# Two graph layers in one kernel: order of layer-norm biases, opening sums, the closing of the last score chain, one load of the diagonal, and where the W1 evacuations stand

## The chip, the cores and the metric

The kernel runs on one core of one Trainium2 chip, in fp32. The metric is device time in microseconds (us), the median of three runs. The profile is of one further execution.

## The reference

Two layers over a graph of 3327 nodes (padded to 26 tiles of 128 rows, 3328) with 512 features and a dense 3327 x 3327 adjacency `adj`:

```
h = relu(layernorm(x));  q = h Wq' + bq;  k = h Wk' + bk;  v = h Wv' + bv
x = x + softmax(q k' / sqrt(512) + adj + adj) v            # layer 0
h = relu(layernorm(x));  A2 = adj + I;  d = diag(A2) ** -0.5
x = x + relu((d A2 d) (A2 h W1'))                           # layer 1
```

## The kernel before, in words

All large matrix products are done in the form of Strassen and Winograd: seven products of half size in place of eight, with sums and differences of blocks made on VectorE. Nodes are split in two halves of 13 tiles (`HALF`), columns in two strips `s` of 14 and 12 tiles (widths `Q` of 448 and 384 in one product). The name of a product (`p1` to `p7`, `m1`) says which blocks it multiplies.

Stage 1, row tiles (to about 110 us). For each tile of x, `norm` (L186) makes statistics on VectorE (`bn_stats` L191, `bn_aggr` L195, `ve` L197), the power -0.5 on GpSimd (L199) and the bias on VectorE (`nb`, L203). ScalarE makes relu(scale x + bias) (`ht`, L321), TensorE transposes it (`tp`, L330) into one of two PSUM banks, ScalarE copies the transposed blocks out (L339 for a tile of the first half, L341 for one of the second), and for the second half VectorE adds blocks (L346, L347). A bank is free again when its copy and its additions are done. `after(ins, other)` gives the builder's scheduler an order on one engine without a semaphore. `adds_of(n)` names the additions of the tile at least three places back in the row order, and `norm` puts the statistics behind them. Between the transposes TensorE makes the projections of q (`project_q`, L451, the merged weight `M`).

Stage 2, scores (about 110 to 622 us). 52 pairs of row tiles: 4 groups (strip and half of the queries) of 13. A pair is a `Chain` of seven products into PSUM rings X, Y and Z (L653); VectorE adds each product into the adjacency tiles g0, g1 (`first` L657, `more` L665), ScalarE takes the exponential (L660, L667), SyncE writes the parts to DRAM (`pd`). A chain's last product, p4, is run in the middle of the next chain (`Chain.finish`), so that it has its bank. Beside each product a fixed list `beside_of(k)` of further work for VectorE is run: the sums s1 to s4 (L675 to L688), `gather` (L699), and the adjacency sums of the next pair (L639, diagonal L643). The block is under `in_order`, which keeps the written order on VectorE, TensorE, GpSimd and SyncE. `at_score[k]` holds loads that are put ahead of pair k.

Stage 3, three large products, `steps`: for g = 0 (softmax times h), 1 and 2 (A2 times something), for each of seven products r, each strip s, seven `t` (six pairs of tiles and one single tile). One step has seven matmuls (L1052) or four (L1043), and needs `a` (loaded by `Step.load`, L1008 and others, three steps ahead), its block sums `o` (`four_sums`, L164 to L166, two steps ahead) and the right side `b` (`Right`, L731, L756, L171 to L174). The views `part` take the memory of `hp`, which the scores read. The loads of steps 0 to 2 and the sums of steps 0 and 1 are written after the scores' block, outside any `in_order`, so the scheduler places them. Between steps further tasks run, put at a step's number by `at(k, what)`; their parts wait in a list `waiting`, of which `run` (L1421 on) lets two go after each matmul while W1 products are inserted. Among these tasks: `totals` and `place_totals` (the softmax sums), `prepare` (Wv, bv and the diagonal `dg`), `prepared` (d from `dg`), `load_diagonal` and `scales` (d again, in blocks of 32 rows, `by_32`, wanted in the last product by `Columns.scale`), `judge` and `judged` (a flag for whether the softmax sums are in range). While step (1, 5, 1, 2) and on run, `Temp.product` (L1220) multiplies by W1: seven small products into two halves of one bank, emptied by ScalarE (L1224) or VectorE (L1226).

The lines above are those of the kernel before. In the kernel after, lines shift by a few (`norm` by 1, the scores by 6), and `left` and `Step` stand ahead of the scores' block.

Of the kernel before, what the change touches and what calls it, by code (L numbers as in the profile page):

```python
# [47 lines left out]
def graph_layers_kernel(  # L48
# [98 lines left out]
    by_32 = const.tile([P, NP // 32], F32, name="by_32")  # L147

# [39 lines left out]
    def norm(src, kept=None, behind=None):  # L188

        st = small.tile([P, 6], F32, name="st")  # L190
        ins = nc.vector.bn_stats(st, src)  # L191
        if behind:
            after(ins, behind)
        mv = small.tile([P, 2], F32, name="mv") if kept is None else kept
        nc.vector.bn_aggr(mv, st)  # L195
        ve = small.tile([P, 1], F32, name="ve")
        nc.vector.tensor_scalar(ve, mv[:, 1:2], EPS, None, op0=ALU.add)  # L197
        rstd = small.tile([P, 1], F32, name="rstd") if kept is None else kept[:, 1:2]
        nc.gpsimd.tensor_tensor(rstd, ve, mhalf, op=ALU.pow)  # L199

        def bias():
            nb = small.tile([P, 1], F32, name="nb")
            nc.vector.scalar_tensor_tensor(nb, mv[:, 0:1], -1.0, rstd, op0=ALU.mult, op1=ALU.mult)  # L203
            return nb

        return rstd, bias
# [107 lines left out]
    def opened(i, behind=None):  # L314
        fetch_x([j for _, j in order].index(i) + 9)
        xt = first.pop(i)
        return xt, *norm(xt, behind=behind)
# [34 lines left out]
    def adds_of(n):  # L352

        return next((summed_up[i] for _, i in reversed(order[: n - 3]) if i in summed_up), None)

    def h_transposed(k, done={}):

        for n, (kk, i) in enumerate(order):
# [4 lines left out]
            else:  # L363
                ht = normal(i, *opened(i, adds_of(n)), behind=taken[order[n - 3][1]])
# [6 lines left out]
    class Turned:  # L371


        def __init__(self, k):
# [3 lines left out]
            for m, (kk, i) in enumerate(order):  # L378
# [4 lines left out]
                rstd, bias = norm(xt, stats[:, :, i // HALF * n + i % HALF - a], adds_of(m))  # L383
# [236 lines left out]
    class Pair:  # L620
# [26 lines left out]
        def multiply(self, qt):  # L647
# [16 lines left out]
            def more(n, ps):  # L664
                nc.vector.tensor_add(a[n], a[n], ps[:, :wd])  # L665
                if n == 1:
                    nc.scalar.activation(g[0], g[0], AF.Exp)  # L667
# [109 lines left out]
    pairs = {}  # L777
    fours = mid(12, [P, 2, Q[0]], "s4")
    steps = [(n, t) for n in range(len(groups)) for t in range(HALF)]

    def fetch(k):
        if k < len(steps):
            pairs[k] = Pair(*steps[k])

    def beside_of(k):
        def on(j, what, *args):
            if 0 <= j < len(steps):
                getattr(pairs[j], what)(*args)

        def difference():  # L790
            if k < len(steps) and steps[k][1] >= 6:
                next(more_of, None)

        return (
            lambda: (on(k - 2, "s4"), on(k - 2, "gather", 0)),
            lambda: (on(k - 1, "s3"), on(k - 2, "gather", 1)),
            lambda: on(k + 1, "sum_of_adjacency", 0),
            lambda: on(k + 1, "sum_of_adjacency", 1),
            lambda: (on(k - 2, "total", 0), difference()),
            lambda: (on(k - 2, "total", 1), on(k - 1, "s1"), next(ahead, None) if k in making else None),  # L800
            lambda: (on(k - 1, "s2"), next(ahead, None) if k in making else None),
        )

    coming = queries(0)
    for ins in more_queries(0, coming):
        if ins:
            after(ins, parts_made[-1])
    for k in range(2):
        fetch(k)
    for m in range(2):  # L810
        pairs[0].sum_of_adjacency(m)
    more_of = iter(())
    with in_order(*(e.engine for e in (nc.vector, nc.tensor, nc.gpsimd, nc.sync))):
        for k, (n, t) in enumerate(steps):
            for what in at_score.get(k, ()):
                what()
            if t == 0:
                qt = coming
            fetch(k + 2)
            if t == 2 and n + 1 < len(groups):  # L820
                coming = queries(n + 1)
                more_of = more_queries(n + 1, coming)
            beside = beside_of(k)
            pairs[k].multiply(qt)
        k = len(steps)
        beside = beside_of(k)
        for what in beside[:2]:
            what()
        Chain.finish()
        for what in (*beside[5:], *beside_of(k + 1)[:2]):  # L830
            what()
        for _ in ahead:
            pass

    def totals():
        for m in range(2):
            pairs[len(steps_of_scores) - 1].total(m)
        for s in range(2):
            y0, y1 = (by_32[:, 4 * (STRIPS[s] + y * HT[s]) : 4 * (STRIPS[s] + (y + 1) * HT[s])] for y in range(2))
            nc.vector.tensor_sub(y0, y0, y1)  # L840

    def place_totals():
        tiled = job_ring([P, P], "tiled")
        for k in range(P // 32):
            nc.vector.tensor_reduce(tiled[:, 32 * k : 32 * k + 32], ident.rearrange("p (a e) -> p e a", e=32), axis=AX.X, op=ALU.add)
        ps = bank(ROLE["p8"], "tot")[:, : 4 * NT]
        nc.tensor.matmul(ps, tiled, by_32, start=True, stop=True)
        ps = ps.rearrange("p (i a) -> p i a", a=4)
        for a in range(4):
            nc.scalar.copy(tot[32 * a : 32 * a + 32, :], ps[32 * a : 32 * a + 32, :, a])  # L850

    steps_of_scores = steps

    ROLE = {"p1": 0, "p6": 2, "p7": 4, "p5": 6, "p2": 7, "p3": 1, "p4": 5, "p8": 3}

    def banks_for(*names):
        return {r: bank(ROLE[r], r) for r in names}

    verdict = []

    def judge():

        if N < NP:
            other = small.tile([P, 1], F32, name="other")
            nc.vector.tensor_sub(other, tot[:, NT - 2 : NT - 1], tot[:, NT - 1 :])
            nc.vector.scalar_tensor_tensor(tot[:, NT - 1 :], other, padding, tot[:, NT - 1 :], op0=ALU.mult, op1=ALU.add)
        within = small.tile([P, NT], F32, name="within")
        nc.vector.tensor_scalar(within, tot, SMALL, None, op0=ALU.is_ge)  # L870
        good = small.tile([P, NT], F32, name="good")
        nc.vector.scalar_tensor_tensor(good, tot, LARGE, within, op0=ALU.is_le, op1=ALU.mult)
        most = small.tile([P, 2], F32, name="most")
        nc.vector.tensor_reduce(most[:, 0:1], tot, axis=AX.X, op=ALU.max)
        nc.vector.tensor_reduce(most[:, 1:2], tot, axis=AX.X, op=ALU.min)
        ps = bank(ROLE["p8"], "p8")
        nc.tensor.matmul(ps[:1, :NT], ones, good, start=True, stop=True)
        for k in range(2):
            nc.tensor.transpose(ps[:1, (k + 1) * P : (k + 2) * P], most[:, k : k + 1], ident)
        verdict.append(ps)  # L880

    def judged():
        ps, one = verdict[0], small.tile([1, 4], F32, name="one")
        nc.vector.reduce_sum(one[:, 0:1], ps[:1, :NT], axis=AX.X)
        nc.vector.tensor_reduce(one[:, 1:2], ps[:1, P : 2 * P], axis=AX.X, op=ALU.max)
        nc.vector.tensor_reduce(one[:, 2:3], ps[:1, 2 * P : 3 * P], axis=AX.X, op=ALU.min)

        nc.vector.scalar_tensor_tensor(one[:, 3:4], one[:, 2:3], RATIO, one[:, 1:2], op0=ALU.mult, op1=ALU.is_ge)
        nc.vector.scalar_tensor_tensor(one[:, 3:4], one[:, 0:1], NT * P - 0.5, one[:, 3:4], op0=ALU.is_ge, op1=ALU.mult)
        nc.vector.tensor_scalar(bad, one[:, 3:4], 0.5, None, op0=ALU.is_lt)  # L890

    sd = const.tile([P, NT], F32, name="sd")
    rs = const.tile([P, NT], F32, name="rs")

    def weights(src):

        w = [half(k, [P, 2, D], "w") for k in (12, 13)]
        for c in range(DC):
            nc.sync.dma_start(w[c // 2][:, c % 2], src[c * P : (c + 1) * P])
        return [w[c // 2][:, c % 2] for c in range(DC)]  # L900

    LD = adjT.shape[1]
    mh = const.tile([P, NT], F32, name="mh")
    nc.vector.memset(mh, -0.5)
    dg = const.tile([P, NT], F32, name="dg")
    bvs = []

    def prepare():
        wv_w1.append(weights(wvT))
        bvs.append(half(11, [P, D], "bv_sb"))  # L910
        nc.sync.dma_start(bvs[0], bass.AP(tensor=bv.tensor, offset=bv.offset, ap=[[0, P], [1, D]]))
        with nc.allow_non_contiguous_dma(reason="the diagonal, once"):
            nc.sync.dma_start(dg, bass.AP(tensor=adjT.tensor, offset=adjT.offset, ap=[[LD + 1, P], [P * (LD + 1), NT]]))

    def load_diagonal():
        with nc.allow_non_contiguous_dma(reason="the diagonal, once"):
            for a in range(4):
# [957 lines left out]
```

## Time and profile before

| | us |
|---|---|
| runs | 2147.93, 2149.40, 2150.25 (median 2149.4) |
| profiled execution | 2149.21 |
| its span, first to last instruction | 2147.4 |
| TensorE granted clock, mean | 0.999 |
| DMA moved | 592 MB, mean 276 GB/s |
| VectorE waiting for DMA of `part` from `p` (13 times) | 26.1 |

The page gives for each engine its busy time, share of the span and number of instructions. Views of the trace are: waits (who waited for whom, in total, times, longest), the timeline (start, length, engine, line, operation, output <- inputs, count of merged instructions; in brackets the idle time before and what ended it), and windows (busy time of each engine in a stretch, then clock, DMA share and GB/s). PE is TensorE's matmul, PEld its weight load, DVE VectorE, ACT ScalarE, POOL GpSimd, SP SyncE. Line numbers are those of the kernel.

### The profile page before, as it was taken

What the parts mean: (1) busy time and instruction counts of PE and PEld (TensorE: products, weight loads), DVE (VectorE), ACT (ScalarE), POOL (GpSimd) and SP (SyncE); (2) the same over time, 40 slices, a digit from 0 to 9 for tenths busy, and PEclk for the clock granted to TensorE, in tenths of its full rate; (3) what the DMA queues carried; (4) which work ended last, traced back from release to release, by engine and by line L of the source; (5) the groups of instructions that cost most, each with busy time, mean ns of one, the idle gap of its engine ahead of it and who ended that gap; (6) DMA issues with size and microseconds to landing.
All of it is one profiled execution on the core that took longest, in us unless ns stands there. A gap on an engine that the chain in (4) does not pass through costs nothing.

```text
span 2147.4 us, 20866 instructions
## 1 busy us (share of the span) xinstructions
PE 2136.9 (100%) x6272; PEld 1180.7 (55%) x6272; DVE 1642.7 (76%) x3214; ACT 273.9 (13%) x441; POOL 68.7 (3%) x63
## 2 busy tenths in 40 slices
PE   9999999999999999999999999999999999999998
PEld 6555555555555555555454555555666665555554
DVE  7579888888887678776777777887466666688888
ACT  6312211112110000001111000000111100000000
POOL 2000000000003000000111000000000000000000
PEclk9999999999999999999999999999999999999999
DMA  8678888888999899888788889886646677978897
GB/s 299 218 258 303 298 312 284 303 291 295 326 339 310 286 350 328 282 303 302 262 310 295 302 284 340 309 314 225 198 157 215 180 212 238 289 225 248 268 280 194
DMA packets 402929, 592.09 MB, mean 276 GB/s; under 512 B 140012, under 2 KB 274296, under 8 KB 402808
## 3 DMA queue, kind: packets, MB, share of 16 engines
q1 hardware_dynamic: 371464, 527.61, 74.6%
q10 hardware_dynamic: 31344, 63.06, 8.0%
q8 instruction: 52, 0.85, 0.2%
q14 instruction: 69, 0.57, 0.1%
HBM read 417.60 MB, written 178.98 MB: 278 GB/s over the span
## 4 chain that ended last, share of the span: by engine, by line
PE 95%; DVE 2%; DMA 2%; issue 0%; ACT 0%; ACTq 0%; SPq 0%; POOL 0%; DVEq 0%
PE p L1052 56%; PE Y L653 13%; PE Z L653 6%; PE p L1043 5%; PE p L1159 4%; PE pw L1220 4%; PE X L653 3%; PE Y L451 2%; PE Z L451 1%; PE X L451 1%; DMA p<-g 0%; DMA bq_sb<-in_bq_dram 0%; DMA part<-p 0%; DMA rows<-row 0%; PE tp L330 0%
## 5 line engine op out<-in xcount | busy, mean ns | idle before, releaser
L1052 PE MATMUL p<-part,b 128*128 128x448 f32 (+1 forms) x3528 | 1257.6, 513 | 0.1
L1052 PEld LDWEIGHTS p<-part,b 128*128 128x128 f32 x3528 | 669.9, 190 | 541.2 <-issue 292.9
L164 DVE TENSOR_TENSOR part<-part 128x896 f32<-128x896 f32 (+1 forms) x252 | 256.5, 1018 | 71.1 <-DMA part<-p 26.1
L653 PE MATMUL Y<-qt,hp 128*128 128x448 f32 (+1 forms) x832 | 308.7, 513 | 0.7 <-DVE g L657 0.6
L653 PEld LDWEIGHTS Y<-qt,hp 128*128 128x128 f32 x832 | 157.7, 190 | 135.0 <-issue 72.8
L653 PE MATMUL Z<-qt,hp 128*128 128x384 f32 (+1 forms) x416 | 162.2, 512 | 0.0
L166 DVE TENSOR_TENSOR part<-part,part 128x448 f32<-128x448 f32 (+1 forms) x219 | 129.4, 591 | 15.0
L165 DVE TENSOR_TENSOR part<-part,part 128x448 f32<-128x448 f32 (+1 forms) x219 | 129.4, 591 | 7.3
L1043 PE MATMUL p<-part,b 128*128 128x448 f32 (+1 forms) x336 | 124.2, 512 | 0.0
L653 PEld LDWEIGHTS Z<-qt,hp 128*128 128x128 f32 x416 | 79.0, 190 | 66.2 <-issue 37.9
L657 DVE SCALAR_TENSOR_TENSOR g<-g,Y 128x384 f32<-128x384 f32 (+1 forms) x156 | 91.4, 586 | 30.5 <-PE Y L653 29.1
L1095 ACT COPY part<-p 128x384 f32<-128x384 f32 (+1 forms) x33 | 16.6, 502 | 658.4 <-PE p L1052 554.9
L1043 PEld LDWEIGHTS p<-part,b 128*128 128x128 f32 x336 | 63.8, 190 | 54.1 <-issue 31.4
L660 ACT ACTIVATE g<-g 128x768 f32<-128x768 f32 (+1 forms) x48 | 43.0, 896 | 346.5 <-DVE g L657 273.5
L653 PE MATMUL X<-qt,hp 128*128 128x384 f32 (+1 forms) x208 | 81.1, 512 | 0.0
L1096 DVE TENSOR_TENSOR part<-p,part 128x384 f32<-128x384 f32 (+1 forms) x33 | 19.3, 586 | 69.5 <-PE p L1052 65.5
L1159 PE MATMUL p<-w,ct 128*128 128x512 f32 x136 | 61.6, 592 | 0.0
L1115 DVE TENSOR_TENSOR ct<-p,part 128x448 f32<-128x448 f32 (+1 forms) x72 | 43.1, 610 | 21.5 <-PE p L1043 16.3
L653 PEld LDWEIGHTS X<-qt,hp 128*128 128x128 f32 x208 | 39.5, 190 | 33.1 <-issue 19.3
L199 POOL TENSOR_TENSOR rstd<-ve,mhalf 128x1 f32<-128x1 f32 x46 | 39.6, 862 | 535.6 <-DVE ve L197 527.0
L1220 PE MATMUL pw<-w,rows 128*128 128x256 f32 x208 | 53.4, 379 | 0.0
L1150 DVE TENSOR_TENSOR job<-job 128x896 f32<-128x896 f32 (+1 forms) x52 | 52.9, 1017 | 0.1
(192 smaller groups left out, 1664.6 us busy)
## 6 DMA issues: line engine op xcount, KB each, us to landing
part<-sum SPq DMA_DIRECT2D x104, 448.0 KB, 4.9
part<-p SPq DMA_DIRECT2D x91, 448.0 KB, 6.1
part<-sum SPq DMA_DIRECT2D x104, 384.0 KB, 3.8
part<-p SPq DMA_DIRECT2D x91, 384.0 KB, 4.3
part<-in_adjT_dram SPq DMA_DIRECT2D x78, 448.0 KB, 4.9
b<-row SPq DMA_DIRECT2D x234, 128.0 KB, 4.8
part<-in_adjT_dram SPq DMA_DIRECT2D x78, 384.0 KB, 3.9
g<-in_adjT_dram SPq DMA_DIRECT2D x52, 448.0 KB, 4.3
```

Source lines behind the costliest of these rows:

```text
L164: yield nc.vector.tensor_add(o[:, 0:2], g[:, 0:4:3], g[:, 1:2].to_broadcast([P, 2, g.shape[-1]]))
L165: yield nc.vector.tensor_add(o[:, 2], o[:, 1], g[:, 0])
L166: yield nc.vector.tensor_add(o[:, 3], o[:, 2], g[:, 2])
L451: nc.tensor.matmul(ps[:, :w], M[B[name]][:, c, o * P : (o + 1) * P], hp[k][:, A[name], c], start=start and c == 0, stop=c == 1, skip_group ...
L653: nc.tensor.matmul(ps[:, :wd], h_of(self.t, name, k), qt[B[name]][:, k], start=start and k == 0, stop=k == 1, skip_group_check=True)
L657: nc.vector.scalar_tensor_tensor(a[n], a[n], 2.0, ps[:, :wd], op0=ALU.mult, op1=ALU.add if sign > 0 else ALU.subtract)
L1043: yield nc.tensor.matmul(ps[("p2", "p3", "p4", "p8")[k]][:, :w], b[:, z], a[:, 0, y], start=k == 3 and not self.seeded, stop=True, skip_gr ...
L1052: yield nc.tensor.matmul(ps[r][:, :w], b[:, i], m, start=self.t == 0 and not adds, stop=self.t == PAIRS - 1 and r in ("p1", "p5", "p6", "p ...
L1115: nc.vector.tensor_tensor(o, p[k], c, op=ALU.subtract if k == "p3" else ALU.add)
L1150: nc.vector.tensor_add(self.a, self.a, self.b)
L1159: nc.tensor.matmul(ps, cts[s][y][d][:, k * P : (k + 1) * P], w[d], start=d == 0, stop=d == DC - 1)
L1220: nc.tensor.matmul(ps, a, W[B[name]][:, c], start=new and c == 0, stop=c == 1, skip_group_check=True)
```

## The change

- `norm` takes two instructions to stand behind: one for the statistics, one for the bias. For tiles from place 13 in the order, the statistics stand behind the additions of the tile five back, the bias behind those three back.
- `left`, `Step`, `view` and the rings move ahead of the scores. The loads of steps 0, 1 and 2 are put at pairs 44, 45 and 46. The six sums of steps 0 and 1 are put at named places of pairs 47 to 51 (`opens`).
- After the scores, `Chain.finish()` comes first, then VectorE's rest.
- `dg` is loaded once, by ScalarE's queue behind an exponential at pair 20. `load_diagonal` of `by_32` (four DMAs), and `scales`, are gone; `place_scales` copies `sd` into `by_32` by 16 ScalarE copies at step 12.
- `prepare` (Wv, bv) moves from step 2 to step (0, 4, 1, 1), number 64. The reductions for `place_totals` move one step up, the verdict's matmuls and the reading of them one step down.
- In `run`, one waiting part instead of two is let go after the second matmul, where a W1 product follows at place 3.

```diff
-    def norm(src, kept=None, behind=None):
+    def norm(src, kept=None, behind=(None, None)):
...
-        if behind:
-            after(ins, behind)
+        if behind[0]:
+            after(ins, behind[0])
...
-            nc.vector.scalar_tensor_tensor(nb, mv[:, 0:1], -1.0, rstd, op0=ALU.mult, op1=ALU.mult)
+            ins = nc.vector.scalar_tensor_tensor(nb, mv[:, 0:1], -1.0, rstd, op0=ALU.mult, op1=ALU.mult)
+            if behind[1]:
+                after(ins, behind[1])
...
-    def adds_of(n):
+    def adds_of(n, back=3):
-        return next((summed_up[i] for _, i in reversed(order[: n - 3]) if i in summed_up), None)
+        return next((summed_up[i] for _, i in reversed(order[: n - back]) if i in summed_up), None)
+    def behind_of(n):
+        return (adds_of(n, 5), adds_of(n)) if n >= HALF else (adds_of(n), None)
...
+    openers = [Step(0, ORDER[0], 0, t, right) for t, right in enumerate(ahead_of)]
+    for n, step in enumerate(openers):
+        at_score.setdefault(44 + n, []).append(step.load)
+    def sums_of_openers():
+        for step in openers[:2]:
+            yield from step.sums()
+    opens, opening = ((47, 4), (48, 4), (49, 4), (50, 4), (51, 2), (51, 3)), sums_of_openers()
...
+    def load_diagonal():
+        step = adjT.shape[1] + 1
+        with nc.allow_non_contiguous_dma(reason="the diagonal, once"):
+            after(nc.scalar.dma_start(dg, bass.AP(tensor=adjT.tensor, offset=adjT.offset, ap=[[step, P], [P * step, NT]])), Pair.exp)
+    at_score.setdefault(20, []).append(load_diagonal)
...
-            lambda: on(k + 1, "sum_of_adjacency", 0),
-            lambda: on(k + 1, "sum_of_adjacency", 1),
-            lambda: (on(k - 2, "total", 0), difference()),
+            lambda: (on(k + 1, "sum_of_adjacency", 0), open_up(2)),
+            lambda: (on(k + 1, "sum_of_adjacency", 1), open_up(3)),
+            lambda: (on(k - 2, "total", 0), difference(), open_up(4)),
...
-        beside = beside_of(k)
-        for what in beside[:2]:
+        Chain.finish()
+        for what in (*beside_of(k)[:2], *beside_of(k)[5:], *beside_of(k + 1)[:2]):
             what()
-        Chain.finish()
-        for what in (*beside[5:], *beside_of(k + 1)[:2]):
-            what()
...
-    def scales():
-        nc.vector.tensor_scalar(by_32, by_32, 1.0, None, op0=ALU.add)
-        nc.gpsimd.tensor_tensor(by_32, by_32, mhalf.to_broadcast(by_32.shape), op=ALU.pow)
+    def place_scales():
+        for a in range(4):
+            to = by_32[32 * a : 32 * a + 32].rearrange("p (i b) -> p b i", b=4)
+            for b in range(4):
+                nc.scalar.copy(to[:, b], sd[32 * b : 32 * b + 32])
...
-    for k, what in ((1, totals), (3, place_totals), (2, prepare), (6, prepared), (5, load_diagonal), (11, scales), (8, judge), (9, judged)):
+    for k, what in ((1, totals), (2, tile_identity), (3, place_totals), (6, prepared), (8, judge), (9, judge_sums), (10, judged),
+                    (12, place_scales), (number_of(0, 4, 1, 1), prepare)):
...
-                do(first_of(waiting), 2)
+                do(first_of(waiting), 1 if j == 2 and (k, 3) in inserted else 2)
```

## The prediction

> **What bounds the kernel now.** I read the page's busy row first, then the waits of TensorE, then the timelines at those waits.
>
> ```profile
> PE 2136.9 (100%) x6272; PEld 1180.7 (55%) x6272; DVE 1642.7 (76%) x3214; ACT 273.9 (13%) x441; POOL 68.7 (3%) x63
> ```
>
> TensorE is never free for long, and the clock row is 9 in all 40 slices. The edits add and remove no matmul, so nothing is to be had but the moments in which TensorE waits. The view of its waits lists few, since it counts idle time after modelled ends:
>
> ```profile
> PE tp L330 <- ACT hp L339: 1.0, 1, 1.0
> PE Y L653 <- DVE g L657: 0.6, 2, 0.3
> PE p L877 <- DVE most L874: 0.5, 1, 0.5
> ```
>
> So I took starts from the timeline instead. Undisturbed passes start every 0.322 us (384 columns), 0.376 (448), 0.216 (256) and 0.109 (transposes); an fp32 matmul is two passes. What a start lies beyond that is lost, and a disturbed pass is mostly followed by 0.10 more. Over the span this gives about 8 us in intervals of more than 0.06. Of it 1.8 is the warm-up on zeros, 0.4 the first projections, 0.4 one wait at 1127.8; none of these is touched. The rest, 5.53 us, is in four places, and each edit aims at one.
>
> Place A, row tiles (26 to 62 us): 0.25 at 34.66, 1.21 at 48.20, 0.09 at 51.78, sum 1.55. TensorE first, then ScalarE:
>
> ```profile
> 46.35 0.81 PE L451 MATMUL Z<-hp,M 128*128 128x384 f32 x2
> 48.20 0.63 PE L330 MATMUL tp<-ident,ht 128*128 128x128 f32 x4 [1.05 <-ACT hp L339]
> ```
>
> ```profile
> 46.92 0.81 ACT L321 ACTIVATE ht<-xt,nb,rstd 128x512 f32<-128x512 f32 x1 [0.56 <-DVE nb L203]
> 47.64 0.56 ACT L339 COPY hp<-tp 128x512 f32<-128x512 f32 x1
> ```
>
> Two passes from 46.35 end their turn at 46.99; the transpose started 1.21 later, when its bank had been copied. The copy stood behind an activation that waited for a bias, whose statistics had been held behind the additions of the tile three back.
>
> Place B, the last five pairs of scores (583 to 623): 0.34, 0.61, 0.38, 0.49, then 0.21 at the first products, sum 2.02. VectorE, then TensorE:
>
> ```profile
> 577.85 0.62 DVE L165 TENSOR_TENSOR part<-part,part 128x448 f32<-128x448 f32 x1
> 579.98 1.09 DVE L164 TENSOR_TENSOR part<-part 128x896 f32<-128x896 f32 x1 [1.52 <-DMA part<-p]
> ```
>
> ```profile
> 588.34 3.23 PE L653 MATMUL Y<-qt,hp 128*128 128x384 f32 x8 [0.34 <-DVE g L657]
> 599.52 1.56 PE L653 MATMUL Y<-qt,hp 128*128 128x384 f32 x4 [0.22 <-DVE g L657]
> ```
>
> An addition of the opening product was put on VectorE before its load (issued at 574.0) had landed. VectorE stood 1.52, then worked without a gap from 580.99 to past 600, and TensorE waited for banks that VectorE reads.
>
> Place C, the verdict, 0.75: two passes of L877 and the transposes started when VectorE's L874/L875 were done.
>
> ```profile
> 663.86 0.21 PE L877 MATMUL p<-good,ones 128*1 128x26 f32 x2 [0.50 <-DVE most L874]
> ```
>
> Place D, times W1 (1572 to 1690): 0.08, 0.08, 0.10, 0.24, 0.36, 0.35, sum 1.21. VectorE, then TensorE:
>
> ```profile
> 1671.38 0.62 DVE L166 TENSOR_TENSOR part<-part,part 128x448 f32<-128x448 f32 x1
> 1671.92 0.68 DVE L756 TENSOR_TENSOR b<-rows 128x512 f32<-128x512 f32 x1
> 1672.52 0.48 DVE L1226 SCALAR_TENSOR_TENSOR ts<-pw,sd,ts 128x256 f32<-128x256 f32 x1
> ```
>
> ```profile
> 1671.30 1.67 PE L1052 MATMUL p<-part,b 128*128 128x448 f32 x4
> 1673.06 1.13 PE L1220 MATMUL pw<-w,ct 128*128 128x256 f32 x4
> ```
>
> The last W1 product was due at 1671.30 + 4 x 0.376 = 1672.81; it needs the half bank that L1226 empties, and L1226 stood behind L756.
>
> **The change, part by part.** Beside the trace I use the order of instructions per engine, as both kernels build.
>
> *D.* In each such step L1226 moves ahead of one addition (L756 or L166: 0.60 to 0.68 from start to start). At 1672 it then starts at 1671.92 and ends at 1672.40, before 1672.81; the largest lateness was 0.25. All go: **1.21** (lower bound 0.9 if a bank release trails). The addition is later by 0.40 and feeds a step two further on, some 10 us.
>
> *C.* The verdict's matmuls go one step later, behind seven products (4.5 us), VectorE's part stays. **0.75**. Its reading by VectorE moves a step too; nobody waits for the flag before the end.
>
> *A.* For the later tiles the statistics are tied behind additions five back, the bias behind three back. I walked the new order with the trace's steps: statistics 0.60, aggregate 0.11, small ones 0.08, additions 0.33 each, activation 0.72, big copy 0.48, half copy 0.28. At 32.71 VectorE now takes two statistics (1.20) ahead of the additions that free a transpose bank; these end at 35.3 instead of 34.51, the transpose comes at 35.46 where it was due at 35.05 (the second Z matmul now precedes it): 0.41 lost instead of 0.25. The 1.21 goes: the activation is ready at 45.75 instead of 46.92, the copy at 46.0, just when TensorE wants the bank. What is late next is the last transpose: its bank's additions wait for a ScalarE copy that stands behind an activation and a projection's copy, and end at 50.3, where TensorE was there at 50.0; with the latency some 0.45. Left 0.9, so gain **0.65**; bounds -0.2 (both lates grow by 0.5) and 1.4.
>
> *B.* Opening sums of steps 0 and 1 stand now at named places of pairs 47 to 51, their loads at pairs 44 to 46, 27 us ahead. The DMA wait of 1.52 is gone. VectorE's step is 0.465 for the 384-wide operations, 0.54 and 1.00 for the sums, 0.21 for a diagonal: pairs 47 and 48 end without lag in their 9.03 us. But the sums of step 2, which the change doesn't name, still float into pairs 49 and 50 in the new order. There VectorE has 9.9 us of work in 9.03. Walking it, the release of the bank for the seventh product of pair 50 ends 0.2 before TensorE wants it; pair 51 has no adjacency sums and catches up. So four waits (1.81) go. The last chain is closed sooner, with two products (1.5 us) ahead of its last matmul, which takes 0.1 away. Then product p3 needs that chain's bank, and its release now stands behind two sums of step 3 (1.5 us, the first waiting for product p5): it would end at about 0.25 after p3 is due, with the restart 0.35 to 0.45. I take 0.45 left in B in all: gain **1.57**, bounds 0.7 (two more waits) and 1.9.
>
> *The diagonal.* Four transfers into `by` (L918), the addition L922 and GpSimd's 17 us are removed, 16 ScalarE copies added, `dg` moves from SP to ScalarE's queue in pair 20, Wv and bv (five loads) to a step near 930 us. Copies: L850 has 0.17 to 0.19 for the same shape, 2.9 us together; ScalarE is 13% busy and nothing behind them there is wanted for tens of us: 0 (2.9 if something were). The `dg` issue took 0.43 on SP, one of L918 took 5.64; it sits between ScalarE's exponentials at 299.0 and 306.75, a gap of 7.7: 0. The transfers themselves:
>
> ```profile
> 557.00:566.00 9.00, 9.00 (x30) 5.29 (x29) 7.87 (x19) 1.69 (x2) 0.00 (x0) 1.00 0.99 338
> 566.00:575.00 9.00, 9.00 (x30) 5.29 (x29) 8.68 (x19) 1.69 (x2) 0.00 (x0) 1.00 0.91 316
> 646.00:654.00 8.00, 8.00 (x23) 4.08 (x22) 5.09 (x9) 0.53 (x1) 0.00 (x0) 1.00 0.98 34
> ```
>
> (Last two columns: DMA share and GB/s.) While L918's 13,312 single elements ran, 34 GB/s moved in 8 us. TensorE lost nothing there, so their removal gives 0. `dg` is a quarter, some 2.3 us of engine time. Read by the row alone, a queue was blocked, and ScalarE's own queue would spare the g loads. The Trainium skill ("DMA: Bandwidth & Descriptors", section "Issuing engines are not separate DMA queues") speaks against that: whichever engine issues, the transfers interleave on the same 16 engines, and only issue time is saved. By the row the g loads lose 0, by the rule up to 2.3; a g tile issued at 568.88 lands 4.3 later (the page's median) and is first read at 575.76, so 2.6 is spare. Either way 0, upper bound 0.5. Wv and bv, 1.3 MB at a share of 0.75 to 1.0, go against loads three steps ahead (15 us): 0.
>
> **Sum.** 1.21 + 0.75 + 0.65 + 1.57 = 4.18. The profiled execution took 2149.21 (span 2147.4 and 1.8 around it): 2145.03. The median, 2149.4, is 0.2 from it, inside its runs' spread, so I keep **2145.0**.
>
> **Rivals.**
> *Everything named is recovered* (A and B without remainder): 5.5 us, 2143.7. For it: pair 50 has the 0.75 of an inserted product as extra room. Against: VectorE's order in A. Chance 0.22.
> *A new wait takes the old one's place*: A gains nothing, p3 and pairs 49 and 50 wait for VectorE: 1.21 + 0.75 + 0.7, 2146.5; the overload of 0.9 in two pairs speaks for it. Chance 0.13.
> *Slower, by DMA in pairs 44 to 46*: two loads of 448 KB instead of one stand ahead of the g loads in SP's queue, at shares of 0.85 to 1.0. Each pair adds 1.3 us of transfer at 350 GB/s; the spare shares are 1.35, 0.1 and 0.8 us, so 1.7 piles up, below the 2.6 of g and 1.8 of VectorE's lead. It decides once g lands 4.4 later than now. Then each of three pairs waits for what is beyond; at a pile of 7, about 2.6 each, 7.8 against 4.2 gained: 2152.8. Chance 0.07.
> *It doesn't do what it says* (the builder's order floats on): 0 to 1, 2149. Chance 0.03.
>
> **How the numbers follow.** A measurement of this kernel tells 0.2% (4.3 us, below 2145.1) from no change. My own case (gain 3.6 to 4.8, chance 0.55) is cut by that border about in half. Faster 0.28 + 0.22 = 0.50; same 0.27 + 0.13 + 0.03 = 0.43; slower 0.07. The range reaches from the full gain, 2143.7, to 2147.3, some way past the second rival.
>
> **What would show it.** A: the transpose at 48.2 starts near 46.1; waits of about 0.4 near 35.4 and 50. B: no DMA wait of L164 near 580, Y without idle time up to the last chain, a short wait of p3 near 621. C: no wait for `most`. D: no passes beyond 0.22 in `pw`. Wrong would be: waits of L639 for `g` near 560, or Y idle over 0.3 near 600.

## The result, and the profile after

The changed kernel takes 2145.33 us (median of 19 runs, 2144.24 to 2145.85), the kernel before 2149.4 (19 runs, 2147.93 to 2150.99). The ratio is 0.9981, with a 95% interval from 0.9975 to 0.9987: 0.13 to 0.25% faster, on both sides of the 0.2% that the prediction took as its border. The forecast was 2145.0. The profiled execution took 2145.52 with a span of 2143.7, 3.7 less than before.

The page's busy row first. TensorE is busy for 1.6 us less with the same 6272 passes; ScalarE has its 16 copies more, GpSimd its long power less.

```profile
PE 2135.3 (100%) x6272; PEld 1182.0 (55%) x6272; DVE 1643.8 (77%) x3213; ACT 277.1 (13%) x457; POOL 53.3 (2%) x62
```

The waits of TensorE (line waited in, releaser, us in total, times, longest):

```profile
PE idle L307 <- DVE mh L1006: 1.1, 1, 1.1
PE p L854 <- DVE g L663: 0.3, 1, 0.3
PE tp L333 <- DVE hp L350: 0.2, 1, 0.2
PE p L854 <- DVE part L1136: 0.2, 1, 0.2
```

The three rows of before (a transpose, Y, and the verdict) are gone. In their place stand two small ones that the prediction named: a transpose that waits for additions, and a product that waits for the last chain's bank. The first row is the start of the span, the last the untouched wait near 1125.

**Row tiles (A).** TensorE's timeline where 1.21 was lost, then the last transpose:

```profile
46.90 0.81 PE L457 MATMUL Z<-hp,M 128*128 128x384 f32 x2
47.55 0.81 PE L457 MATMUL X<-hp,M 128*128 128x384 f32 x2
48.19 0.27 PE L333 MATMUL tp<-ident,ht 128*128 128x128 f32 x1
...
50.69 0.63 PE L333 MATMUL tp<-ident,ht 128*128 128x128 f32 x4 [0.17 <-DVE hp L350]
```

From 46.90 to 48.19 every group starts when the passes before it have run. The builder has put two of X's passes (0.64) ahead of this transpose, so it comes at 48.19 and not near 46.1 as forecast, but nothing is lost on the way. (46.1 does not fit the prediction's own lines either: by them the transpose was due at 46.99.) What frees its bank shows on VectorE, before and then after:

```profile
47.24 0.16 DVE L203 SCALAR_TENSOR_TENSOR nb<-mv,rstd 128x1 f32<-128x1 f32 x1 [0.36 <-POOL rstd L199]
47.31 0.41 DVE L346 TENSOR_TENSOR hp<-hp,tp 128x256 f32<-128x256 f32 x1
47.65 0.41 DVE L347 TENSOR_TENSOR hp<-hp,tp 128x256 f32<-128x256 f32 x1
```

```profile
47.50 0.41 DVE L350 TENSOR_TENSOR hp<-hp,tp 128x256 f32<-128x256 f32 x1
47.83 0.15 DVE L204 SCALAR_TENSOR_TENSOR nb<-mv,rstd 128x1 f32<-128x1 f32 x1
```

The two banks take turns, so this transpose needs the bank of the tile two back, which the additions L346 and L347 (L349 and L350 after) read last. In the kernel before they ended at 48.06, and the transpose started 0.14 later. The same 0.14 or 0.15 lies between the end of such additions and the late transposes at 34.66 before and at 35.86 and 50.69 after. So the additions released it. The view of before names the copy L339, which ended at the same moment but empties the other bank. The additions stood behind two biases that waited 0.59 (at 46.72) and 0.36 for GpSimd's power. In the changed kernel the biases stand behind the additions. These end at 47.91, and TensorE was done with Z at 47.55: without X's passes in between, some 0.5 would still be lost (an estimate from these rows).

At 50.69 the transpose is 0.34 late: it was due 2 x 0.322 after the start of the Y passes at 49.71.

**End of the scores (B).** VectorE's waits between 560 and 620 us, all there are:

```profile
DVE g L671 <- PE Z L659: 1.5, 2, 0.7
DVE g L685 <- ACT g L666: 0.5, 1, 0.5
DVE g L663 <- PE Y L659: 0.4, 2, 0.3
```

The 1.5 us for a load is gone, and no Y product is late. What is left is p3. VectorE, then TensorE:

```profile
617.87 1.09 DVE L165 TENSOR_TENSOR part<-part 128x896 f32<-128x896 f32 x1
618.99 0.62 DVE L166 TENSOR_TENSOR part<-part,part 128x448 f32<-128x448 f32 x1
619.53 0.55 DVE L663 SCALAR_TENSOR_TENSOR g<-g,Y 128x384 f32<-128x384 f32 x1
```

```profile
618.96 0.92 PE L854 MATMUL p<-part,b 128*128 128x448 f32 x2
620.14 1.77 PE L854 MATMUL p<-part,b 128*128 128x448 f32 x4 [0.27 <-DVE g L663]
```

Two passes from 618.96 make p3 due at 619.71; it starts at 620.14, since L663 frees the bank only after two sums of a later step. That costs 0.43, and 0.10 at the pass after it.

**Verdict (C).** VectorE's comparisons are over at 660.26, long before TensorE comes:

```profile
660.00 0.17 DVE L974 TENSOR_REDUCE most<-tot 128x1 f32<-128x26 f32 x1
```

```profile
665.67 0.21 PE L980 MATMUL p<-good,ones 128*1 128x26 f32 x2
```

**W1 (D).** This is the same place in the step as the one shown of before. L1247 now stands ahead of L762; the W1 product starts 4 x 0.376 after the passes before it, to the hundredth:

```profile
1668.89 0.48 DVE L1247 SCALAR_TENSOR_TENSOR ts<-pw,sd,ts 128x256 f32<-128x256 f32 x1
1669.28 0.68 DVE L762 TENSOR_TENSOR b<-rows 128x512 f32<-128x512 f32 x1
```

```profile
1668.27 1.67 PE L854 MATMUL p<-part,b 128*128 128x448 f32 x4
1669.77 1.03 PE L1241 MATMUL pw<-w,ct 128*128 128x256 f32 x4
```

**The diagonal.** The stretch in which 34 GB/s moved at a DMA share of 0.98 (last column GB/s, before it the share):

```profile
646.00:654.00 8.00, 8.00 (x24) 4.21 (x23) 5.63 (x10) 0.00 (x0) 0.00 (x0) 1.00 0.64 224
```

Counted as the prediction counts (starts of TensorE later than the pitch by more than 0.06 us), the four places lose 0.51, 0.53, 0.18 and 0.17, in all 1.39 where it was 5.53: 4.14 recovered. The profiled execution of after lost 0.80 more in the first projections, where nothing was changed (the last section returns to this). Of the 3.7 by which its span is shorter, this count explains 3.34; the rest lies in delays too small for it. The medians differ by 4.07.

### The profile page after: what moved, and what is told of

It reads as the page before. It is cut to its first block, busy times and chain, and to the rows that moved or that the text cites. A ratio compares the mean times of both kernels' runs of the same rounds, so it can differ in the third digit from the quotient of the medians.

```text
span 2143.7 us, 20871 instructions
## 1 busy us (share of the span) xinstructions
PE 2135.3 (100%) x6272; PEld 1182.0 (55%) x6272; DVE 1643.8 (77%) x3213; ACT 277.1 (13%) x457; POOL 53.3 (2%) x62
## 4 chain that ended last, share of the span: by engine, by line
PE 98%; DVE 1%; DMA 0%; ACT 0%; issue 0%; DVEq 0%; ACTq 0%
PE p L854 57%; PE Y L659 13%; PE Z L659 7%; PE p L845 5%; PE p L1180 4%; PE pw L1241 4%; PE X L659 3%; PE Y L457 2%; PE Z L457 1%; PE mm L499 1%; PE X L457 0%; PE tp L333 0%; DMA row<-h 0%; PE idle L307 0%; DVE st L192 0%
## 5 line engine op out<-in xcount | busy, mean ns | idle before, releaser
L165 DVE TENSOR_TENSOR part<-part 128x896 f32<-128x896 f32 (+1 forms) x252 | 256.7, 1019 | 65.4 <-DMA part<-sum 21.3
L166 DVE TENSOR_TENSOR part<-part,part 128x448 f32<-128x448 f32 (+1 forms) x219 | 129.4, 591 | 7.3
L663 DVE SCALAR_TENSOR_TENSOR g<-g,Y 128x384 f32<-128x384 f32 (+1 forms) x156 | 91.5, 586 | 29.8 <-PE Y L659 26.4
```

The lines of the kernel that those rows point to most:

```text
L165: yield nc.vector.tensor_add(o[:, 0:2], g[:, 0:4:3], g[:, 1:2].to_broadcast([P, 2, g.shape[-1]]))
L166: yield nc.vector.tensor_add(o[:, 2], o[:, 1], g[:, 0])
L663: nc.vector.scalar_tensor_tensor(a[n], a[n], 2.0, ps[:, :wd], op0=ALU.mult, op1=ALU.add if sign > 0 else ALU.subtract)
```

## The experiments

All start from the changed kernel. The four places of each are counted in the one profiled execution; the time is the median of 11 runs (19 of before and after), with the ratio to the kernel before on the same chip. The experiments ran on three chips, on which the kernel before has medians of 2149.04 to 2149.17; so differences of a few tenths between medians say nothing. "First projections" counts what is lost from 4.8 to 20 us.

| kernel | us | ratio, 95% interval | A | B | C | D | first projections |
|---|---|---|---|---|---|---|---|
| before | 2149.40 | | 1.55 | 2.02 | 0.75 | 1.21 | 0.41 |
| after | 2145.33 | 0.9981 (0.9975 to 0.9987) | 0.51 | 0.53 | 0.18 | 0.17 | 1.21 |
| undo_a | 2145.99 | 0.9984 (0.9975 to 0.9993) | 1.43 | 0.53 | 0.18 | 0.10 | 1.27 |
| undo_c | 2145.10 | 0.9980 (0.9971 to 0.9989) | 0.63 | 0.53 | 0.18 | 0.10 | 0.84 |
| undo_d | 2146.45 | 0.9987 (0.9978 to 0.9996) | 0.52 | 0.53 | 0.18 | 1.23 | 0.95 |
| b_late | 2146.60 | 0.9989 (0.9980 to 0.9998) | 0.49 | 2.80 | 0.18 | 0.21 | 1.03 |
| b_free | 2145.20 | 0.9980 (0.9971 to 0.9989) | 0.56 | 0.32 | 0.18 | 0.10 | 0.85 |
| b_close | 2146.56 | 0.9988 (0.9979 to 0.9997) | 0.50 | 1.75 | 0.18 | 0.10 | 1.03 |
| b_pile | 2146.57 | 0.9988 (0.9979 to 0.9997) | 0.62 | 4.93 | 0.18 | 0.10 | 0.67 |
| dg_sp | 2145.26 | 0.9980 (0.9971 to 0.9989) | 0.63 | 0.54 | 0.18 | 0.10 | 0.63 |
| elements_c | 2145.15 | 0.9981 (0.9971 to 0.9990) | 0.50 | 0.53 | 0.18 | 0.10 | 1.18 |
| wv_c | 2145.12 | 0.9982 (0.9973 to 0.9991) | 0.51 | 0.53 | 0.18 | 0.10 | 0.86 |
| both | 2145.19 | 0.9981 (0.9972 to 0.9990) | 0.50 | 0.53 | 0.18 | 0.10 | 1.23 |
| better | 2145.67 | 0.9982 (0.9973 to 0.9991) | 1.08 | 0.31 | 0.18 | 0.10 | 0.00 |

The intervals, which carry the spread of the kernel before, overlap almost everywhere. On one chip the runs themselves part the larger differences: all of b_close (2146.03 to 2146.89) are longer than all of b_free and dg_sp (at most 2145.72). For the rest, the place in the trace tells the kernels apart. Where an edit does not reach it, it repeats to a few hundredths in B and C (C is 0.18 in all 13) and within 0.15 in A and D. The medians serve as a check on the size.

### One edit undone

**undo_a**

```
-        return (adds_of(n, 5), adds_of(n)) if n >= HALF else (adds_of(n), None)
+        return (adds_of(n), None)
```

> The changed kernel with the row tiles' part alone undone (statistics behind the additions three back, biases free). Theory (each edit is worth what TensorE lost at its own place, and the places add): the wait of 1.2 us for a transpose near 48 to 49 us comes back, that near 35 grows to 0.25, the one near 50.7 (0.34) goes; row tiles lose 1.55 instead of 0.50, the other places stay; 1.05 more than the changed kernel's 2145.3, so 2146.4. Rival (the gain came from the whole order before the scores, not from the biases): the place loses 0.5 to 0.8 as now, 2145.3 to 2145.6.

The wait came back, 1.21 at 48.80, with the same VectorE picture as before: the additions stand behind a bias that waits for GpSimd, and end at 48.65, where the changed kernel ends them at 47.91 (TensorE is at the same point within 0.05 in both). On TensorE, X's passes stand behind this transpose again.

```profile
47.83 0.16 DVE L204 SCALAR_TENSOR_TENSOR nb<-mv,rstd 128x1 f32<-128x1 f32 x1 [0.36 <-POOL rstd L200]
47.91 0.41 DVE L349 TENSOR_TENSOR hp<-hp,tp 128x256 f32<-128x256 f32 x1
48.24 0.41 DVE L350 TENSOR_TENSOR hp<-hp,tp 128x256 f32<-128x256 f32 x1
```

A is 1.43 (0.14, 1.21, 0.08) against 0.51: 0.92 in the trace, 0.66 in the medians. The theory that the places add holds here; the rival falls.

**undo_c**

```
-(8, judge), (9, judge_sums), (10, judged)
+(8, judge), (8, judge_sums), (9, judged)
```

> The changed kernel with the verdict's matmuls back in the step of its comparisons. Theory: TensorE waits 0.66 plus 0.09 for most at about 662 us; 0.18 is there now, so 0.57 more, 2145.9. Rival (0.75 was the shapes' own cost and not a wait): no difference from the changed kernel at this place, 2145.3.

Nothing came back. The verdict's matmuls stand where they stood in the kernel before and lose 0.09 and 0.09, as in all the others; the time is 2145.10. VectorE, then TensorE:

```profile
659.83 0.17 DVE L974 TENSOR_REDUCE most<-tot 128x1 f32<-128x26 f32 x1
```

```profile
660.98 0.21 PE L980 MATMUL p<-good,ones 128*1 128x26 f32 x2
```

Here the comparisons are done about 0.9 before TensorE comes; in the kernel before, TensorE stood 0.50 for them. So the theory fell, and the rival does not do either: the kernel before did lose 0.66 to a wait. Something else in the change brought VectorE forward. Three kernels further down look for it.

**undo_d**

```
-do(first_of(waiting), 1 if j == 2 and (k, 3) in inserted else 2)
+do(first_of(waiting), 2)
```

> The changed kernel with the W1 additions back to two per place. Theory: the late starts of the W1 products between 1568 and 1686 us come back, 0.08, 0.08, 0.10, 0.24, 0.36 and 0.35, 1.21 in all against 0.17 now: 1.04 more, 2146.4. Rival (the moved addition only shifts the wait to another product): 0.5 or less of difference, 2145.3 to 2145.8.

All six late starts returned (0.08, 0.08, 0.10, 0.24, 0.36 and 0.36), D is 1.23, the median 1.12 above the changed kernel's. L762 is ahead of L1247 again, and the W1 product due at 1668.36 + 4 x 0.376 = 1669.86 starts at 1670.12:

```profile
1668.99 0.68 DVE L762 TENSOR_TENSOR b<-rows 128x512 f32<-128x512 f32 x1
1669.59 0.48 DVE L1247 SCALAR_TENSOR_TENSOR ts<-pw,sd,ts 128x256 f32<-128x256 f32 x1
```

```profile
1668.36 1.67 PE L854 MATMUL p<-part,b 128*128 128x448 f32 x4
1670.12 1.13 PE L1241 MATMUL pw<-w,ct 128*128 128x256 f32 x4
```

### The opening sums, taken apart

**b_late**: no loads at pairs 44 to 46, no places for the sums; the closing stays.

```
-    for n, step in enumerate(openers):
-        at_score.setdefault(44 + n, []).append(step.load)
...
-opens, opening = ((47, 4), (48, 4), (49, 4), (50, 4), (51, 2), (51, 3)), sums_of_openers()
+opens, opening = (), sums_of_openers()
...
+    for step in openers:
+        step.load()
     for what in early:
         for _ in what() or ():
             pass
+    for _ in opening:
+        pass
```

> The changed kernel with the opening layer's loads and sums back where the builder's order let them float; the sooner closing of the last chain stays. Theory: VectorE stands about 1.5 us for a load near 576 us, then has no idle time, and TensorE waits in three or four Y products between 580 and 597 us, 1.4 to 1.8 in all, besides the wait at p3 (0.5); so 1.5 more, 2146.8. Rival (what cured B was the sooner closing): no Y waits over 0.2, 2145.3.

VectorE, then TensorE:

```profile
580.21 1.09 DVE L165 TENSOR_TENSOR part<-part 128x896 f32<-128x896 f32 x1 [2.40 <-DMA part<-p]
```

```profile
584.09 2.85 PE L659 MATMUL Y<-qt,hp 128*128 128x384 f32 x8 [0.96 <-DVE g L663]
```

VectorE stands 2.40 for the load in this execution, and four Y products lose 2.69 with their restarts; p3 loses only 0.10. B is 2.80; the median is 1.27 above the changed kernel's. The sooner closing did not cure this.

**b_free**: the loads stay at pairs 44 to 46, the sums are where the builder puts them (as in b_late).

> The changed kernel with the opening loads kept at pairs 44 to 46, but the sums of steps 0 and 1 not placed: the builder puts them. Theory (the load that came too late was the cause): VectorE waits for no DMA near 576, Y products lose 0.3 or less, p3 waits about as now (0.5); place B loses 0.5 to 0.9, 2145.3 to 2145.7. Rival (where the sums stand is what counts, since three sums of 2 us each fall together): Y products lose 1.0 or more between 580 and 610, 2146.3 to 2147.

No DMA wait of VectorE, 0.21 in one Y product, 0.10 in the last chain, none at p3: B is 0.32, the time 2145.20. So the earlier load is the whole cure, and naming the sums' places adds nothing. Without the places VectorE is even ahead at p3. Its release there stands behind no sum and waits for TensorE. TensorE's order differs too: two products, as in the kernel before, stand between the chain's last passes and p3, where the changed kernel has one, so that there p3 is due 0.75 sooner. VectorE in b_free:

```profile
618.48 0.55 DVE L663 SCALAR_TENSOR_TENSOR g<-g,Y 128x384 f32<-128x384 f32 x1 [1.18 <-PE Y L659]
```

**b_close**: only the closing of the last chain as before.

```
-        Chain.finish()
-        for what in (*beside_of(k)[:2], *beside_of(k)[5:], *beside_of(k + 1)[:2]):
+        beside = beside_of(k)
+        for what in beside[:2]:
+            what()
+        Chain.finish()
+        for what in (*beside[5:], *beside_of(k + 1)[:2]):
```

> The changed kernel with only the closing of the scores' last chain undone: TensorE's order stays, on VectorE the release of the bank that p3 takes stands behind four more operations (4 x 0.465). Theory: p3 near 620 starts 1.3 to 1.9 later than now: wait of 1.7 to 2.3 instead of 0.53, 2146.6 to 2147.2. Rival (the release was early enough either way, as in the kernel before, which lost only 0.21 there): 0.2 to 0.5 lost, 2145.0 to 2145.3.

```profile
621.16 2.15 PE L854 MATMUL p<-part,b 128*128 128x448 f32 x5 [1.48 <-DVE g L663]
```

p3 starts 1.64 late instead of 0.43; the median is 1.23 above. On VectorE four operations of 0.465 now stand between L165 and L663, where the changed kernel has one L166. The sooner closing is worth 1.2, but only in the new order; the kernel before, without it, lost 0.21. The rows say why. Before, the release ended 1.48 after the chain's last passes had run (622.12 for 620.64) and p3 was due 1.50 after them. Here it ends 2.34 after them, a sum (L165) being ahead of it, and p3 is due 0.75 sooner, with one product in between and not two.

### The transfers

**b_pile**: all three opening loads at pair 45.

```
-        at_score.setdefault(44 + n, []).append(step.load)
+        at_score.setdefault(45, []).append(step.load)
```

> The changed kernel with all three opening loads (six transfers of 448 KB, 2.7 MB, 7.7 us at 350 GB/s) at pair 45, ahead of the g loads of pair 47. It brings about the pile that the rival 'slower, by DMA' needs. That rival: g of pair 47 lands more than 4.4 us later than now, and the sum of adjacency and the Y products behind it wait, 1 to 5 us in all, 2146.5 to 2150. The other view (the transfers spread over the engines and VectorE's lead takes the rest): g lands 3 to 4 us later, no wait of TensorE, 2145.3.

The two g loads behind the six transfers land 9.1 and 9.6 us after their issue, where the changed kernel has 4.3 to 5.7 (four g loads, 555 to 575 us). VectorE stands 4.04 for them:

```profile
569.57 0.56 DVE L645 TENSOR_TENSOR o<-g 128x384 f32<-128x384 f32 x1 [4.04 <-DMA g<-in_adjT_dram]
```

TensorE stands still for 2.06 and then runs at half rate for a while; the windows (the column after the five engines is the granted TensorE clock):

```profile
568.00:570.60 2.60, 0.59 (x2) 0.00 (x0) 1.03 (x3) 0.00 (x0) 0.00 (x0) 1.00 1.06 395
570.60:574.30 3.70, 3.65 (x6) 2.04 (x7) 2.99 (x7) 1.58 (x2) 0.00 (x0) 0.54 0.91 341
```

B is 4.93 here: 2.22 for the wait, 1.80 for six passes that start 0.2 to 0.3 late at the lower clock, 0.91 at p3. This execution was among the longest, 2149.62; the eleven runs reach from 2145.10 to 2149.91, so the wait is probably long in some and short in others; only this one has a profile. The rival "slower, by DMA" is real at such a pile. In the change itself, with one load a pair, nothing of it is seen: no wait for g, DMA share 1.04 in both stretches from 557 to 575.

**dg_sp**: the diagonal's load on SP's queue, `nc.sync.dma_start(dg, ...)` for `nc.scalar.dma_start(dg, ...)`.

> The changed kernel with the diagonal's load on SP's queue in front of the g loads of pair 22, instead of ScalarE's queue. Theory (as forecast, the transfers share the same engines whichever queue issues them, and only 0.4 us of issue time changes): the g loads behind it land 0 to 1 us later than now, no TensorE wait over 0.06 near 300, 2145.3. Rival (single elements in front block the queue): the g loads behind it land 2 us or more later, and if VectorE's lead of 1.8 is used up a wait appears, up to 0.5; 2145.3 to 2145.8.

The two g loads behind it take 1.91 to issue instead of 0.89. They land 4.6 and 4.8 after their issue, where the changed kernel has 4.0 and 5.1, and TensorE loses nothing near 300. At this place the queue costs only issue time, as the rule that the prediction cited says.

### What healed the verdict

The order of instructions on VectorE around the comparisons is the same in the kernel before and in undo_c. What differs is when they run. The kernel before, VectorE's sums ahead of the comparisons:

```profile
644.87 0.96 DVE L164 TENSOR_TENSOR part<-part 128x768 f32<-128x768 f32 x1 [4.62 <-DMA part<-p]
...
660.74 0.96 DVE L164 TENSOR_TENSOR part<-part 128x768 f32<-128x768 f32 x1 [0.75 <-DMA part<-p]
```

They waited for loads (a third 0.54 at 657.84), and the comparisons behind them began only at 662.87. SP's queue in the kernel before (time in the second column is what the issues took):

```profile
634.30 0.43 SPq L913 DMA_DIRECT2D dg<-in_adjT_dram  x1
634.99 6.44 SPq L1008 DMA_DIRECT2D part<-p  x5
641.52 10.29 SPq L918 DMA_DIRECT2D by<-in_adjT_dram  x4
651.92 3.44 SPq L1008 DMA_DIRECT2D part<-p  x4
```

The first of the five loads behind `dg` took 4.33 to issue, and the next loads after L918 were issued only from 651.92. So the transfers that the change took away were suspected of the wait. Three kernels put them back.

**elements_c** (four single-element loads on SP in step 5, into the table that the scales are copied to later, and the verdict's matmuls in the old place):

```
-(3, place_totals), (6, prepared), (8, judge), (9, judge_sums), (10, judged)
+(3, place_totals), (5, load_elements), (6, prepared), (8, judge), (8, judge_sums), (9, judged)
```

> The changed kernel with the verdict's matmuls back in the step of its comparisons and with the four single-element loads of the diagonal back on SP (into the table that the scales are later copied to). What undo_c left open: with the old place of the matmuls there was no wait. Theory now: the wait for most came from the sums ahead of the comparisons, which waited for loads that stood behind L918's elements; so VectorE's sums between 643 and 662 wait for DMA again (0.5 to 4 us each), the comparisons come up to 3 us later, and the verdict's matmuls wait 0.3 to 0.7 beyond the 0.18 that is always there: 2145.4 to 2145.8. Rival (the elements cost nothing there, as forecast): 0.18 at the verdict, 2145.1.

**wv_c** (Wv and bv loaded in step 2 as before, the matmuls in the old place):

```
-(12, place_scales), (number_of(0, 4, 1, 1), prepare)
+(12, place_scales), (2, prepare)
```

> The changed kernel with the verdict's matmuls back in the step of its comparisons and with Wv's and bv's five loads (1.3 MB) back in front of the opening layer's later loads. If these and not the elements held the loads up: VectorE waits for DMA between 640 and 662 and the verdict's matmuls wait 0.3 to 0.7 more, 2145.4 to 2145.8. If they are made good within the 15 us after them (the theory here): a wait of VectorE near 640, none after 655, 0.18 at the verdict, 2145.1.

**both** (both sets of loads back, the matmuls a step later as in the change).

> The changed kernel (matmuls of the verdict a step later) with both the single elements and Wv's loads back in the old places. Theory: VectorE's comparisons come at about 662 to 664 as in the kernel before, the matmuls only at about 666, so the move alone is enough: 0.18 at the verdict, 2145.3, unless some other product waits for the late sums (each up to 0.5). Rival (the move does nothing under the old queue): 0.75 at the verdict, 2145.9.

In none of the three did the comparisons come late: L974 starts at 659.97, 659.66 and 660.01, and C is 0.18. The kernel `both`, with both sets of loads back, is the telling one. SP's queue and VectorE's only DMA wait in that stretch:

```profile
631.61 7.19 SPq L810 DMA_DIRECT2D part<-p  x5
638.89 7.44 SPq L1018 DMA_DIRECT2D by<-in_adjT_dram  x4
646.44 3.64 SPq L810 DMA_DIRECT2D part<-p  x4
```

```profile
639.80 0.96 DVE L165 TENSOR_TENSOR part<-part 128x768 f32<-128x768 f32 x1 [1.50 <-DMA part<-p]
```

The loads after the elements are issued from 646.44, 5.5 earlier than in the kernel before, and land in time. So the second theory fell as well in the form it had: neither the elements nor Wv, alone or together, bring the wait back. Two things of the old queue are in none of these three kernels. One is `dg` on SP between Wv and the next loads; the first load behind it took 4.33 to issue, where `both` has 0.33. The other is the later loads of the opening steps. They alone are not it: in b_late, which has them, VectorE waits for no load here, and the comparisons end as long before TensorE comes as in the changed kernel (5.40 and 5.41). That `dg`, alone or together with the other loads, made VectorE late fits the rows but was not tried. Because the wait never came back, it is also untested whether moving the matmuls would have been enough by itself. By the rows of before it would: 4.5 later than 663.20, where they were due, is well behind 663.89, where the comparisons ended.

### A version that might beat both

**better**: b_free, and the statistics behind the additions four back, `(adds_of(n, 4), adds_of(n))`.

> The changed kernel with two edits: the sums of the opening steps not placed (their loads stay at pairs 44 to 46), and the statistics of the later row tiles behind the additions four back instead of five. Theory: the wait for p3 near 620 goes (place B 0.3 instead of 0.53) and the one near 35.8 goes (row tiles 0.35 instead of 0.5), the one near 50.5 stays since it hangs on ScalarE's copy; 0.35 less, 2145.0. Rival (the statistics four back make the activations late again): 0.5 or more lost between 40 and 52, 2145.5 or more.

The rival was right. B is 0.31, but A rose to 1.08. With the statistics that close, VectorE's bias waits for GpSimd's power again, and the additions that free a bank stand behind it; the transpose at 50.24 loses 0.53:

```profile
49.28 0.16 DVE L204 SCALAR_TENSOR_TENSOR nb<-stats 128x1 f32<-128x1 f32 x1 [0.53 <-POOL stats L200]
```

The median is 2145.67. So five back for the statistics is the better choice here, and no version tried is measurably faster than the changed kernel: b_free is 0.13 below it, and its trace 0.21 better in B.

## Why the prediction was right, and where not

Its sum, 4.18, met the 4.14 of the trace and the 4.07 of the medians. That it fits so closely is luck: A gave 0.39 more than forecast, and B, C and D together 0.43 less. The terms one by one:

- **D**, 1.21 forecast. Recovered 1.04 in the profile of after, 1.12 in time when undone. Mechanism right. The 0.17 left are a start of 0.10 near 1560, which is in nearly all these kernels but not in before, and one of 0.07.
- **A**, 0.65 forecast, 1.04 in the trace, 0.92 when undone. The 1.21 went, but the step that explained it was wrong: "The copy stood behind an activation that waited for a bias". The copy is that of the other bank. What TensorE waited for were VectorE's additions, which stood behind two biases themselves, and "the copy at 46.0, just when TensorE wants the bank" did not happen: the bank is free at 47.91, and X's passes fill the time until then. The two waits that the prediction walked out are there, but smaller: 0.17 near 35.9 for 0.41, 0.34 near 50.7 for 0.45. The mis-sized term is "0.41 lost instead of 0.25". This wait is 0.29 in the profiled executions that lost 0.63 to 0.84 in the first projections, and 0.16 or 0.17 in seven of the eight that lost 0.85 or more (0.22 in b_free), undo_a and better aside. The execution from which it was worked out had lost 0.41 there.
- **B**, 1.57 forecast, 1.49 in the trace. The four Y waits went, p3 waits 0.53 with its restart where 0.35 to 0.45 was said, for the reason that was said (two sums ahead of its release, and a product more ahead of the chain's last matmul). The overload of 0.9 in pairs 49 and 50 caused no wait. What the working did not separate: the loads at pairs 44 to 46 do all of it (b_free). Naming the sums' places brings the wait at p3, and the sooner closing, given "0.1", is worth 1.2 in that order (b_close).
- **C**, 0.75 forecast, 0.57 in the trace. Here the step failed although the size is close. It said "The verdict's matmuls go one step later, behind seven products (4.5 us), VectorE's part stays". VectorE's part did not stay: L974 runs 3.6 us sooner than L874 did (660.00 for 663.63), of which 1.7 is what the scores end sooner; and undo_c shows that the move was not needed. And 0.18 of the 0.75 was no wait; it is there in every kernel.
- **The diagonal**, 0 forecast: "TensorE lost nothing there, so their removal gives 0". That looked only at the stretch of the transfers and only at TensorE. Between 640 and 661 us VectorE waited 4.62, 0.58, 0.54 and 0.75 for loads, and so came late to the comparisons that TensorE waited for until 663.86; that was booked under C. As far as the rows show, the loads' timing made C's wait; which of the edits ended it, the runs do not settle.
- **The rivals.** "Everything named is recovered" did not happen: 1.39 is left. "A new wait takes the old one's place" was right in kind (p3, the two transposes) and gave back 1.0 in these three. "Slower, by DMA" needs a pile that the change does not make; b_pile made it and lost 4.9 in its profiled execution. "It doesn't do what it says" is out.

## What to carry to other kernels

Follow a wait back until it ends at something that cannot be helped: the comparisons were late because sums were late, because loads were late, and the edit that looks like the cure (move the waiting matmul) may not be the one that acts. The releaser that a view names is inferred: where two engines end at the same moment, work out which of them held the buffer. Of a transfer that costs its own stretch nothing, ask who waits for the loads queued behind it, and where that engine is next needed. When several edits are worth 1 us each in 2145, count late starts by place in the trace: undoing one edit at a time tells them apart there, where the intervals of the time hardly do.

## What the runs showed of the hardware

A stand of 2.06 us on TensorE (b_pile) was followed by passes at half rate: 0.64 from start to start instead of 0.32, with a granted clock of 0.54 from 570.6 to 574.3. Stands of 1.05 us (before) and 1.48 us (b_close) were not. The Trainium skill ("TensorE: Matmul & The Clock Gate", section "Part 1: The HAM clock gate") says that the clock falls after an idle window of about 3.4 us; here 2.06 was enough, in the one execution that shows it.

The clock matters at the start too. The two profiled executions, 4.7 to 7.3 us, before and then after:

```profile
4.70:7.30 2.60, 2.60 (x8) 1.20 (x7) 0.00 (x0) 0.00 (x0) 0.00 (x0) 1.00 1.00 281
```

```profile
4.70:7.30 2.60, 2.60 (x6) 1.11 (x5) 0.48 (x1) 0.00 (x0) 0.00 (x0) 1.00 0.94 287
```

In before the first projections run at full rate at once (about 0.43 a pass), in after three passes take 0.79 to 0.86 each, about twice that, though the granted clock reads 1.00 in both. The 16 warm-up passes ahead are the same. Over the profiled executions the full rate came between about 3.3 us (b_pile) and 6.1 us (undo_a) after the first pass, whatever the edit, and half-rate passes cost the first projections between 0.00 and 1.26. One profiled execution can so differ from another by as much as one of these edits is worth, which is a reason to compare place by place.
